# A prologue in another order: first weights earlier, score columns as products of their own, products of ones, factors per 128 rows

## The chip, the cores and the metric

The kernel runs on one core of a Trainium2 chip (trn2). The core has a matrix engine (TensorE, PE in the profile; its weight loads are shown as PEld), three engines for elementwise work (VectorE or DVE, ScalarE or ACT, GpSimd or POOL), and SyncE (SP), whose queue issues every transfer (DMA) of this kernel between device memory and the on-chip buffers. The engines run their own instruction streams, each in strict order, and wait for each other by semaphores. The metric is the device time of one execution in microseconds (us); lower is better.

## The reference

Two graph layers over 64 batches of 256 nodes with 512 features, in fp32. Cut to what matters:

```python
h = relu(layernorm(x))                       # layer 0
hW = einsum('bnf,fo->bno', h, W)             # W: 512 x 256
e = hW @ a[0] + swapaxes(hW @ a[1], 1, 2)    # score columns, one per node
alpha = softmax(leaky_relu(e, 0.2) + NEG * (1 - adj))
x = x + concatenate([alpha @ hW, hW], -1)

h = relu(layernorm(x))                       # layer 1, 8 heads of 64
q, k, v = h @ Wq.T + bq, h @ Wk.T + bk, h @ Wv.T + bv
attn = softmax(where(adj == 0, -inf, q @ k.T / 8))
x = x + (attn @ v) @ Wo.T + bo
```

## The kernel before, in words

The 64 batches are worked in 32 groups of two (`g`, with `b` 0 or 1); a batch is two tiles of 128 rows, so a group has four tiles `r`. All loops are unrolled. Each stage is a Python generator that emits one piece of instructions per `next`, and the order of the pieces is written out by hand: the first lines behind `verdict = judge()` (L1072 to L1126) are the prologue, the strings `steps` (L1131) the steady loop. There, each group's attention is interleaved with the projections of the group after it and with layer 0 of the group two ahead. The order on PE is pinned (`in_order`, L131); `not_sooner` (L123) pins an instruction behind the last one that was emitted on its engine.

The stages that matter here:

- `load(g, b)` (L147) transfers a batch of x, 512 KB.
- `first_norm(g)` (L531) normalizes for layer 0. `stats` computes mean and variance of 128 rows on DVE (BATCH_NORM_STATS2 and AGGREGATE), `factors` makes of them the scale and offset (two DVE operations, a power and a product on POOL, `factor`), `norm` applies them on ScalarE (`xn`). `turn`, `fetch` and `put` turn the result so that features lie on partitions (`hT`). For group 0 this goes through PE (transposes `pt` against `ident`). For all others it goes through memory: DVE transposes blocks of 32 (`xt`), SP stores them (`passed`, one transfer), SP fetches them back rearranged (`moved`, four transfers, which wait for `passed`), ScalarE copies them (`hT<-moved`).
- `first_layer(g)` (L671) is the rest of layer 0. For groups 0 and 1, four feature tiles `ph` are computed with `w0_sb`, which holds W in columns 2 to 257 and the two score columns W a[0], W a[1] in columns 0 and 1. `score_columns` (L174) computes these on DVE in eight products (`prod`). ScalarE copies a tile to `H`. The scores `e`: group 0 transposes score columns on PE (`pn`), later groups take them through memory (`score_rows`, L596: DVE transposes to `rows`, then transfers `line` and `own`). ScalarE adds and exponentiates, DVE multiplies by the mask `maskT`, PE computes the weighted sums `po`, DVE normalizes them into x and takes the statistics for layer 1.
- `project(g)` (L793) computes q, k and v of a group in seven block products each (Strassen-Winograd), from `hT` of layer 1, its `sums` (POOL) and the `sums` of the weights.
- `judge` (L292) computes bounds of the weights in pieces, among them `gram_q`, `gram_k` and four squares on PE. `mask` (L183) makes `maskT`.
- `late_loads` (L229) issues 19 transfers on SP: x of group 2 (2), the output weights `wo_sb` (8), the value bias `bv_col` (8) and the output bias `b_out` (1), each pinned behind SP's last.

Before the change SP issues in this order: x of group 0 (both batches), a_b (the vectors a), W, adj, Wq, x of group 1, Wk, biases, Wv, then `passed` and `moved` of group 1's first batch, of its second batch, then `late_loads`, then `line`, x of group 3, `own`. PE's order in the prologue: transposes of group 0's first batch, `ph` 0 and 1, transposes of the second, the mask's, `ph` 2 and 3, `pn`, gram_q, four `po`, gram_k, `ph_1_0` and `ph_1_1` (group 1), layer 1's transposes, squares, first q products.

Of the kernel before, what the change touches and what calls it, by code (L numbers as in the profile page):

```python
# [14 lines left out]
P = 128  # L15
# [42 lines left out]
def bounded(  # L58
# [86 lines left out]
    xs = {}  # L145

    def load(g, b):  # L147
        xs[g, b] = big.tile([P, NT, D], F32, tag="x", name=f"x{g}_{b}", bufs=8)
        if g == 2:
            not_sooner(sync, "dma_start", xs[g, b], xg[g, b])  # L150
        else:
            sync.dma_start(xs[g, b], xg[g, b])

    load(0, 0)
    load(0, 1)


    ident = const.tile([P, P], F32, name="ident")
    make_identity(nc, ident)
    maskT = const.tile([P, NT, N], F32, name="maskT")  # L160
    bad = const.tile([P, 2, NT], F32, name="bad")
    a_b = big.tile([P, 2, F1], F32, tag="oT0", name="a_b", bufs=1)
    nc.sync.dma_start(
        a_b, bass.AP(tensor=a0.tensor, offset=a0.offset, ap=[[0, P], [F1, 2], [1, F1]])
    )

    w0_sb = const.tile([P, HP, F1 + 2], F32, name="w0_sb")
    nc.sync.dma_start(w0_sb[:, :, 2:], w0.rearrange("(c p) o -> p c o", p=P))
    FH = F1 // 2 + 1
# [13 lines left out]
    def mask():  # L183
        edge = att.tile([P, NT, N], F32, tag="kept", name="edge", bufs=3)
        not_sooner(vector, "tensor_scalar", edge, adj_i, 0.0, None, op0=ALU.not_equal)
        yield
        pt = mm("pt_mask").rearrange("p (k q) -> p k q", k=NT)
        for kb in range(NT):
            for t in range(NT):
                transpose(  # L190
                    pt[:, kb, t * P : (t + 1) * P], edge[:, t, kb * P : (kb + 1) * P], ident
                )
        not_sooner(vector, "tensor_copy", maskT, pt)

        not_sooner(vector, "reduce_max", bad[:, 0, :], edge, axis=AX.X)
        vector.tensor_scalar(bad[:, 0, :], bad[:, 0, :], 0.0, None, op0=ALU.is_equal)
        vector.tensor_tensor(edge, edge, adj_i, op=ALU.not_equal)
        vector.reduce_max(bad[:, 1, :], edge, axis=AX.X)
        yield
# [52 lines left out]
    gpsimd.memset(ones, 1.0)  # L252
    square_ones = const.tile([P, P], F32, name="square_ones")
    gpsimd.memset(square_ones, 1.0)

    def weight_sums(name, engine=vector):
# [35 lines left out]
    def judge():  # L292
# [16 lines left out]
        for n, name in enumerate(("q", "k")):  # L309
            gram = bank(f"gram_{name}")  # L310
            for hp in range(HP):
                half, cols = hp // 2, slice(hp % 2 * P, (hp % 2 + 1) * P)
                for c in range(HP):
                    w = w_sb[name][:, c % 2, c // 2 * 2 + half, cols]
                    matmul(gram[:, hp, :], w, w, start=(c == 0), stop=(c == HP - 1))
            power[name] = room[:, n * HP : (n + 1) * HP, :]
            vector.tensor_mul(
                power[name], gram, heads[:, None, :].to_broadcast([P, HP, P])
            )
            yield  # L320
        for i in range(2):
            for n, name in enumerate(("q", "k")):
                square = bank(f"square_{name}{i}")
                for hp in range(HP):
                    a = power[name][:, hp, :]
                    matmul(square[:, hp, :], a, a, start=True, stop=True)
                if i < 1:
                    not_sooner(scalar, "copy", power[name], square)
                else:
                    scalar.activation(  # L330
                        power[name], square, AF.Square, accum_out=part[:, 8 + n : 9 + n]
                    )
                yield

# [87 lines left out]
    def norm_T(src, mv, name, by_pe):  # L422
# [5 lines left out]
        J = P // S  # L428

        def factors(b):  # L430
            tiles = slice(b * NT, (b + 1) * NT)
            several = small.tile([P, 3, NT], F32, tag="factor", name=f"factor{name}_{b}")
            ve, less, rstd = (several[:, i, :] for i in range(3))
            vector.tensor_scalar(ve, mv[:, tiles, 1], EPS, None, op0=ALU.add)
            vector.tensor_scalar(less, mv[:, tiles, 0], -1.0, None, op0=ALU.mult)
            if name == "0_0" or (name, b) == ("0_3", 0):
                not_sooner(gpsimd, "tensor_tensor", rstd, ve, rexp, op=ALU.pow)
            else:
                gpsimd.tensor_tensor(rstd, ve, rexp, op=ALU.pow)
            gpsimd.tensor_tensor(less, less, rstd, op=ALU.mult)  # L440
            factor[b] = less, rstd

        def norm(b):
            less, rstd = factor[b]
            for t in range(NT):
# [57 lines left out]

        return factors, norm, turn, fetch, put

# [25 lines left out]
    def first_norm(g):  # L531
# [5 lines left out]
        def measure(b):  # L537
            for t in range(NT):
                xt[b * NT + t] = xs[g, b][:, t, :]
                stats(mv, xt, b * NT + t, f"0_{g}")  # L540
            factors(b)

# [3 lines left out]

        if g in (1, 2):
            for b in range(GB):
                measure(b)
                yield  # L550
        if g == 1:
            for b in range(GB):
# [8 lines left out]
            return  # L561
        for b in range(GB):
            if g != 2:
# [6 lines left out]
            if g == 0:  # L570
                to_operand(b)
        if g == 0:
            return
# [97 lines left out]
    def first_layer(g):  # L671

        xt = [xs[g, b][:, t, :] for b in range(GB) for t in range(NT)]
        if g > 1:
            yield from first_products(g)
        for r in range(GT if g <= 1 else 0):
            b, t = divmod(r, NT)
            ph = mm(f"ph_{g}_{r}")[:, : F1 + 2]
            for c in range(HP):
                matmul(  # L680
                    ph, hT0[g, b][:, c, t * P : (t + 1) * P], w0_sb[:, c, :],
                    start=(c == 0), stop=(c == HP - 1),
                )
            scalar.copy(H[:, r, : F1 + 2], ph)
            gpsimd.tensor_add(xt[r][:, F1:], H[:, r, 2 : F1 + 2], xt[r][:, F1:])
            if r < GT - 1:
# [40 lines left out]
        for r in range(GT):  # L727
            b, t = divmod(r, NT)
            po = mm(f"po_{g}_{r}")[:, : F1 + 1]
            for kb in range(NT):  # L730
# [5 lines left out]
            not_sooner(vector, "reciprocal", ri, po[:, F1:])  # L736
            vector.scalar_tensor_tensor(
                xt[r][:, :F1], po[:, :F1], ri, xt[r][:, :F1], op0=ALU.mult, op1=ALU.add
            )
            stats(mv, xt, r, f"1_{g}")  # L740
            if r == 1:
                factors(0)
            elif r == 2:
                norm(0)
            elif r == 3:
                factors(1)
                if g:
# [45 lines left out]
    def project(g):  # L793
        ops = operands.pop(g)
        for name in ("q", "k", "v"):
# [25 lines left out]
            def take(to, bank, half):  # L821

                behind = [scalar.last] if g <= 1 and name != "v" else []
                if name == "v":
# [249 lines left out]
    bias, edges = last_bias(), mask()  # L1074
    for piece in range(5):
        next(norms)
        if piece == 3:
            score_columns()
            next(edges)
    products, pieces = project(0), first_layer(1) if NG > 1 else iter(())  # L1080
    for piece, _ in enumerate(first_layer(0)):
        if piece == 1:
            for _ in range(3):
                next(norms)
            next(edges)
        elif piece == 2 or piece == 3:
            next(norms)
        elif piece == 4:
            next(verdict)
            next(norms)  # L1090
        elif piece == 5:
            next(norms)
            late_loads()
        elif piece == 7:
            next(norms)
        elif piece == 9:
            next(verdict)
            next(pieces)
            next(pieces)
        elif piece == 10:  # L1100
            next(verdict)
            next(verdict)
            weight_sums("q")
        elif piece == 11:
            next(products)
            next(products)
            next(norms)
    next(norms)
    next(norms)
    next(pieces)  # L1110
    next(pieces)
    next(verdict)
    next(verdict)
    order = "- n s n s - - ss ss s s n - n - s - s -".split()
    for i, parts in enumerate(order, 2):
# [7 lines left out]
        for part in parts:  # L1123
            if part != "-":
                next(norms if part == "n" else pieces, None)
        if i in (12, 18, 19):  # L1126
            next(bias)
# [5 lines left out]
    for g in range(NG):  # L1133
        products = project(g + 1) if g + 1 < NG else iter(())
        pieces = first_layer(g + 2) if g + 2 < NG else iter(())
        for b, parts in enumerate(steps):
# [9 lines left out]
            for part in parts:  # L1146
# [409 lines left out]
```

## Time and profile before

| what | us |
|---|---|
| median of three runs (lowest, highest) | 2398.05 (2397.5, 2398.47) |
| the profiled execution's own time | 2401.28 |
| its span | 2399.5 |
| PE busy in 0 to 10, 10 to 20, 20 to 30 | 1.79, 8.12, 9.86 |
| DVE busy in the same windows | 4.09, 7.71, 8.91 |
| PE busy in 60 to 70, 100 to 110, 120 to 130 | 9.48, 9.05, 8.00 |
| PE busy in 1000 to 2000 | 1000.00 |

The profile is one execution, taken by the hardware profiler; its times count from the start of the span. In the steady part a group takes about 73 us (the scores of consecutive batches begin at 161.60, 198.82 and 234.97) and PE has no gap there. One fp32 matmul product is recorded as two matmuls, a transpose as one. Waits and releasers are inferred from semaphores; where an engine's order is strict, whatever stands behind a waiting instruction waits with it.

### The profile page before, as it was taken

Reading aid. Unit: us, or ns where it says so; the run is one execution under the profiler, and the core shown is the slowest. Engines: PE = TensorE matmul, PEld = TensorE weight load, DVE = VectorE, ACT = ScalarE, POOL = GpSimd, SP = SyncE. Lnnn points to the kernel's source line nnn. Section 1 sums busy time; section 2 is a strip of 40 time slices with the busy share of each in tenths; the row PEclk is TensorE's granted clock in tenths of the full one; section 3 lists DMA queues with packets and bytes.
Section 4 is the critical chain, followed back from the end, with each engine's and each line's share of the span. In section 5 each row is a group of like instructions: output and inputs, shape, how many; then the busy total and the mean of one; then the engine's idle time right before and its main releaser. Section 6 shows DMA issues by size and latency. Waiting matters only on the chain.

```text
span 2399.5 us, 42951 instructions
## 1 busy us (share of the span) xinstructions
PE 2378.2 (99%) x15772; PEld 2005.0 (84%) x15772; DVE 1693.1 (71%) x3338; ACT 1021.4 (43%) x2017; POOL 1418.4 (59%) x1282
## 2 busy tenths in 40 slices
PE   8999999999999999999999999999999999999998
PEld 7878888888888888888888888888888888888886
DVE  6677776777766777666767667776667676677666
ACT  5444444444443444444444434444444444344331
POOL 3565566656657555666556565655665555655652
PEclk9999999999999999999999999999999999999999
DMA  6344445544454544454444545444544445454331
GB/s 202 109 141 152 125 148 157 150 149 142 137 154 150 162 149 135 137 162 150 146 145 136 155 150 164 145 135 139 162 150 146 145 136 154 150 163 142 111 99 46
DMA packets 272041, 343.76 MB, mean 143 GB/s; under 512 B 25424, under 2 KB 217168, under 8 KB 271824
## 3 DMA queue, kind: packets, MB, share of 16 engines
q1 hardware_dynamic: 271824, 340.95, 46.0%
q8 instruction: 126, 2.06, 0.4%
q14 instruction: 91, 0.75, 0.1%
HBM read 177.22 MB, written 163.64 MB: 142 GB/s over the span
## 4 chain that ended last, share of the span: by engine, by line
PE 96%; DMA 1%; DVE 1%; ACT 1%; POOL 0%; issue 0%; SPq 0%; ACTq 0%; DVEq 0%; POOLq 0%
PE pv L137 16%; PE pk L137 16%; PE py L137 16%; PE pq L137 16%; PE sc L137 10%; PE pr L137 9%; PE ph L137 8%; PE po L137 4%; DMA x<-in_x_dram 0%; SPq L35 0%; DMA w_sb<-in_L_gnn_W_dram 0%; ACT e L35 0%; DMA line<-rows 0%; POOL x L35 0%; POOL parts L35 0%
## 5 line engine op out<-in xcount | busy, mean ns | idle before, releaser
L35 POOL TENSOR_TENSOR p<-p 128x512 f32<-128x512 f32 x248 | 384.5, 1563 | 483.4 <-DVE p L35 465.0
L35 ACT ACTIVATE xn<-x,factor 128x512 f32<-128x512 f32 x256 | 194.5, 807 | 324.5 <-POOL factor L35 324.0
L35 DVE TENSOR_TENSOR p<-p,maskT 128x1024 f32<-128x1024 f32 x254 | 329.5, 1318 | 1.4 <-ACT p L35 1.4
L35 ACT ACTIVATE p<-sc 128x512 f32<-128x512 f32 x512 | 258.1, 627 | 138.9 <-PE sc L137 121.1
L35 DVE TENSOR_TENSOR x<-py,x 128x256 f32<-128x256 f32 x448 | 185.8, 415 | 183.3 <-PE py L137 177.1
L35 POOL TENSOR_TENSOR parts<-parts 128x512 f32<-128x512 f32 x248 | 248.0, 1000 | 86.4 <-DMA parts<-rows 62.7
L137 PE MATMUL py<-wo_sb,oT 128*128 128x256 f32 x1024 | 262.4, 379 | 0.6 <-DVE oT L35 0.6
L137 PE MATMUL sc<-q,k 64*128 64x256 f32 x2048 | 253.1, 391 | 2.0 <-DVE oT L35 2.0
L137 PEld LDWEIGHTS sc<-q,k 64*128 64x128 f32 x2048 | 205.6, 187 | 50.1 <-issue 26.3
L137 PE MATMUL pk<-hT,wk_sb 128*128 128x256 f32 x1024 | 244.8, 382 | 0.0
L137 PE MATMUL pq<-hT,wq_sb 128*128 128x256 f32 x1024 | 240.0, 382 | 0.3 <-ACT kept_q L35 0.3
L137 PE MATMUL pv<-wv_sb,hT 128*128 128x256 f32 x1024 | 236.9, 379 | 0.0
L137 PE MATMUL pr<-p,v 128*32 128x256 f32 x4096 | 234.2, 380 | 0.0
L35 POOL TENSOR_TENSOR factor<-factor,rexp 128x2 f32<-128x2 f32 x128 | 115.6, 903 | 179.9 <-DVE factor L35 179.7
L137 PEld LDWEIGHTS pq<-hT,wq_sb 128*128 128x128 f32 x1024 | 191.8, 190 | 35.8 <-issue 10.3
L137 PEld LDWEIGHTS py<-wo_sb,oT 128*128 128x128 f32 x1024 | 194.2, 190 | 28.2 <-DVE oT L35 1.1
L137 PEld LDWEIGHTS pk<-hT,wk_sb 128*128 128x128 f32 x1024 | 189.7, 190 | 33.3 <-issue 9.9
L137 PEld LDWEIGHTS pv<-wv_sb,hT 128*128 128x128 f32 x1024 | 194.5, 190 | 27.1 <-issue 0.5
L137 PEld LDWEIGHTS pr<-p,v 128*32 128x32 f32 x4096 | 126.8, 110 | 97.8 <-issue 15.9
L137 PE MATMUL py<-wo_sb,o_sums 128*128 128x256 f32 x768 | 197.6, 380 | 1.4 <-DVE x L35 1.3
L137 PE MATMUL pk<-sums,wk_sb 128*128 128x256 f32 x768 | 181.6, 379 | 0.5 <-ACT kept_k L35 0.5
L137 PE MATMUL pq<-sums,wq_sb 128*128 128x256 f32 x768 | 181.4, 379 | 0.0
(148 smaller groups left out, 4059.1 us busy)
## 6 DMA issues: line engine op xcount, KB each, us to landing
passed<-xt SPq DMA_DIRECT2D x124, 512.0 KB, 3.1
moved<-passed SPq DMA_DIRECT2D x496, 128.0 KB, 3.5
rows<-p SPq DMA_DIRECT2D x124, 512.0 KB, 3.4
parts<-rows SPq DMA_DIRECT2D x496, 128.0 KB, 3.0
x<-in_x_dram SPq DMA_DIRECT2D x64, 512.0 KB, 4.4
out_dram<-x SPq DMA_DIRECT2D x62, 512.0 KB, 4.0
own<-line SPq DMA_DIRECT2D x31, 256.0 KB, 3.2
wq_sb<-in_L_gnn_Wq_dram SPq DMA_DIRECT2D x2, 512.0 KB, 9.9
```

The lines of the kernel that those rows point to most:

```text
L35: instruction = getattr(self.engine, operation)(*args, **kwargs)
L137: in_order(nc.tensor.matmul(*args, **kwargs))
```

## The change

Nothing that is computed for the output changes but the way to the two score columns of group 0's first batch; the rest is order.

1. PE begins with 12 products of ones (`warm_up`) into a bank that nobody reads; `square_ones` is set earlier.
2. SP's order: W directly behind the first batch of x, then the second batch, then a_b. x of group 3 is issued in the prologue, behind a `passed` of group 2.
3. For group 0's first batch, the 256 feature columns and the 2 score columns are products of their own, the latter emitted behind the transposes of the second batch.
4. Scale and offset are computed per 128 rows in group 0, for both layers (`factor_of`), no longer per 256.
5. Group 1's normalization is emitted later: its ScalarE part behind group 0's exponentials, its DVE transposes behind the product that follows gram_q. Between its two batches, on SP, now stand the 19 transfers of `late_loads`.
6. On PE: gram_k moves ahead of the fourth `po`; the feature tiles of group 1 (`ph_1_0` to `ph_1_3`) move behind layer 1's transposes and between the q products; the squares move behind the last q product and behind the second k product.
7. The last residual addition is emitted at the end of the step before.

```diff
+    def warm_up():
+        warm = mm("warm")
+        for _ in range(12):
+            matmul(warm[:, :P], square_ones, square_ones, start=True, stop=True)
...
     load(0, 0)
-    load(0, 1)
+    square_ones = const.tile([P, P], F32, name="square_ones")
+    gpsimd.memset(square_ones, 1.0)
...
+    w0_sb = const.tile([P, HP, F1 + 2], F32, name="w0_sb")
+    nc.sync.dma_start(w0_sb[:, :, 2:], w0.rearrange("(c p) o -> p c o", p=P))
+    load(0, 1)
     a_b = big.tile([P, 2, F1], F32, tag="oT0", name="a_b", bufs=1)
...
+        def factor_of(b, t):
+            if t == 0:
+                several = small.tile([P, 3, NT], F32, tag="factor", name=f"factor{name}_{b}")
+                factor[b] = several[:, 0, :], several[:, 1, :], several[:, 2, :]
+            less, rstd, ve = (f[:, t : t + 1] for f in factor[b])
+            r = b * NT + t
+            not_sooner(vector, "tensor_scalar", ve, mv[:, r, 1:2], EPS, None, op0=ALU.add)
+            not_sooner(vector, "tensor_scalar", less, mv[:, r, 0:1], -1.0, None, op0=ALU.mult)
+            not_sooner(gpsimd, "tensor_tensor", rstd, ve, rexp[:, :1], op=ALU.pow)
+            gpsimd.tensor_tensor(less, less, rstd, op=ALU.mult)
...
+        apart = NT if g == 0 else 0
+        heads = []
+        for r in range(apart):
+            heads.append(mm(f"ph_{g}_{r}")[:, : F1 + 2])
+            features(heads[r], r, slice(2, F1 + 2), True)
+            yield
+        for r in range(apart):
+            features(heads[r], r, slice(0, 2), False)
+            taken(heads[r], r)
...
-    for piece in range(5):
-        next(norms)
-        if piece == 3:
-            score_columns()
-            next(edges)
...
-    order = "- n s n s - - ss ss s s n - n - s - s -".split()
+    work = {"n": norms, "0": layer, "1": pieces, "u": products, "c": verdict, "e": edges}
+    warm_up()
+    take(*"nnnnn")
+    score_columns()
+    take(*"en00nn0e00n0cnn")
+    late_loads()
+    take(*"000n0c00n0n")
+    weight_sums("q")
+    take(*"euun0011")
+    order = "- nss n nn ns - s - ss ss s s n - n - s - s".split()
...
+        if i in (6, 8):
+            take(*"cc")
+        if i == 7:
+            take("c")
+        if i == 8 and NG > 3:
+            load(3, 0)
+            load(3, 1)
...
-                parts = ("Smmoomoomooo", "Smrmoomoomooo")[b]
+                parts = ("Smmoomoomooor", "Smmoomoomooo")[b]
...
-                    if g + 3 < NG:
+                    if 0 < g < NG - 3:
```

In the strings, a letter is one piece of a stage: n of the normalizations, 0 and 1 of layer 0 for groups 0 and 1, u of group 0's projections, c of `judge`, e of `mask`, s of group 1's layer, and in the loop's strings S the scores, m the masking, o the outputs, r a residual addition.

More of the change, by code (lines that the diff above doesn't have):

```diff
@@ L145, in bounded @@
     xs = {}
+    def warm_up():
+        warm = mm("warm")
+        for _ in range(12):
+            matmul(warm[:, :P], square_ones, square_ones, start=True, stop=True)
     def load(g, b):
         xs[g, b] = big.tile([P, NT, D], F32, tag="x", name=f"x{g}_{b}", bufs=8)
-        if g == 2:
+        if g in (2, 3):
             not_sooner(sync, "dma_start", xs[g, b], xg[g, b])
@@ L165, in bounded @@
     )
-    w0_sb = const.tile([P, HP, F1 + 2], F32, name="w0_sb")
-    nc.sync.dma_start(w0_sb[:, :, 2:], w0.rearrange("(c p) o -> p c o", p=P))
     FH = F1 // 2 + 1
@@ L252, in bounded @@
     gpsimd.memset(ones, 1.0)
-    square_ones = const.tile([P, P], F32, name="square_ones")
-    gpsimd.memset(square_ones, 1.0)
     def weight_sums(name, engine=vector):
@@ L316, in judge @@
             power[name] = room[:, n * HP : (n + 1) * HP, :]
-            vector.tensor_mul(
-                power[name], gram, heads[:, None, :].to_broadcast([P, HP, P])
+            not_sooner(
+                vector, "tensor_mul", power[name], gram, heads[:, None, :].to_broadcast([P, HP, P])
             )
             yield
+        squared = {}
         for i in range(2):
@@ L327, in judge @@
                 if i < 1:
-                    not_sooner(scalar, "copy", power[name], square)
+                    squared[name] = square
                 else:
@@ L332, in judge @@
                     )
+                yield
+            for name, square in squared.items():
+                not_sooner(scalar, "copy", power[name], square)
+            if squared:
+                squared.clear()
                 yield
@@ L435, in factors @@
             vector.tensor_scalar(less, mv[:, tiles, 0], -1.0, None, op0=ALU.mult)
-            if name == "0_0" or (name, b) == ("0_3", 0):
+            if (name, b) == ("0_3", 0):
                 not_sooner(gpsimd, "tensor_tensor", rstd, ve, rexp, op=ALU.pow)
@@ L443, in norm @@
         def norm(b):
-            less, rstd = factor[b]
+            less, rstd = factor[b][:2]
             for t in range(NT):
@@ L502, in put @@
             put_last[:] = [scalar.last]
-        return factors, norm, turn, fetch, put
+        return (factor_of if by_pe else factors), norm, turn, fetch, put
     def operand_sums(engine, quads, sums):
@@ L540, in measure @@
                 stats(mv, xt, b * NT + t, f"0_{g}")
-            factors(b)
+                if g == 0:
+                    factors(b, t)
+            if g:
+                factors(b)
         def to_operand(b):
@@ L545, in to_operand @@
             put(b, hT0[g, b])
-        if g in (1, 2):
+        if g == 1:
             for b in range(GB):
@@ L550, in first_norm @@
                 yield
-        if g == 1:
-            for b in range(GB):
                 norm(b)
@@ L561, in first_norm @@
             return
+        if g == 2:
+            for b in range(GB):
+                measure(b)
+                yield
         for b in range(GB):
@@ L571, in first_norm @@
                 to_operand(b)
+                yield
         if g == 0:
@@ L675, in first_layer, with features, taken @@
             yield from first_products(g)
-        for r in range(GT if g <= 1 else 0):
+        def features(ph, r, columns, start):
             b, t = divmod(r, NT)
-            ph = mm(f"ph_{g}_{r}")[:, : F1 + 2]
             for c in range(HP):
                 matmul(
-                    ph, hT0[g, b][:, c, t * P : (t + 1) * P], w0_sb[:, c, :],
-                    start=(c == 0), stop=(c == HP - 1),
+                    ph[:, columns], hT0[g, b][:, c, t * P : (t + 1) * P], w0_sb[:, c, columns],
+                    start=start and c == 0, stop=(c == HP - 1), skip_group_check=(g == b == 0),
                 )
+        def taken(ph, r):
             scalar.copy(H[:, r, : F1 + 2], ph)
-            gpsimd.tensor_add(xt[r][:, F1:], H[:, r, 2 : F1 + 2], xt[r][:, F1:])
+            sum_of = xt[r][:, F1:], H[:, r, 2 : F1 + 2], xt[r][:, F1:]
+            if g:
+                not_sooner(gpsimd, "tensor_add", *sum_of)
+            else:
+                gpsimd.tensor_add(*sum_of)
+        apart = NT if g == 0 else 0
[3 more added lines that the diff above has]
+            features(heads[r], r, slice(2, F1 + 2), True)
+            yield
+        for r in range(apart):
+            features(heads[r], r, slice(0, 2), False)
+            taken(heads[r], r)
+        if apart:
+            yield
+        for r in range(apart, GT if g <= 1 else 0):
+            ph = mm(f"ph_{g}_{r}")[:, : F1 + 2]
+            features(ph, r, slice(0, F1 + 2), True)
+            taken(ph, r)
             if r < GT - 1:
@@ L736, in first_layer @@
             not_sooner(vector, "reciprocal", ri, po[:, F1:])
-            vector.scalar_tensor_tensor(
-                xt[r][:, :F1], po[:, :F1], ri, xt[r][:, :F1], op0=ALU.mult, op1=ALU.add
-            )
-            stats(mv, xt, r, f"1_{g}")
-            if r == 1:
-                factors(0)
-            elif r == 2:
+            weighed = xt[r][:, :F1], po[:, :F1], ri, xt[r][:, :F1]
+            if g == 0:
+                not_sooner(
+                    vector, "scalar_tensor_tensor", *weighed, op0=ALU.mult, op1=ALU.add
+                )
+            else:
+                vector.scalar_tensor_tensor(*weighed, op0=ALU.mult, op1=ALU.add)
+            stats(mv, xt, r, f"1_{g}")
+            if g == 0:
+                factors(b, t)
+            elif t == 1:
+                factors(b)
+            if r == 2:
                 norm(0)
             elif r == 3:
-                factors(1)
                 if g:
@@ L821, in take @@
             def take(to, bank, half):
-                behind = [scalar.last] if g <= 1 and name != "v" else []
+                behind = [scalar.last] if g == 0 and name != "v" else []
                 if name == "v":
@@ L1074, in bounded, with take @@
     bias, edges = last_bias(), mask()
-    for piece in range(5):
-        next(norms)
-        if piece == 3:
-            score_columns()
-            next(edges)
[L1080 to L1113, printed above, removed]
-    order = "- n s n s - - ss ss s s n - n - s - s -".split()
+    def take(*names):
+        for name in names:
+            next(work[name])
+    layer, products = first_layer(0), project(0)
+    pieces = first_layer(1) if NG > 1 else iter(())
+    work = {"n": norms, "0": layer, "1": pieces, "u": products, "c": verdict, "e": edges}
[8 more added lines that the diff above has]
+    order = "- nss n nn ns - s - ss ss s s n - n - s - s".split()
     for i, parts in enumerate(order, 2):
```

## The prediction

> **What bounds the kernel now.** I read the page first: TensorE (PE) is busy for 2378.2 of 2399.5 us, so all other time is 21 us of PE gaps, and only a gap on PE can be won or lost.
>
> ```profile
> PE 2378.2 (99%) x15772; PEld 2005.0 (84%) x15772; DVE 1693.1 (71%) x3338; ACT 1021.4 (43%) x2017; POOL 1418.4 (59%) x1282
> ```
>
> The busy times by window (window, length, then busy us and records of PE, PEld, DVE, ACT and POOL, granted clock, DMA share, GB/s) say where the gaps are: 8.2 + 1.9 us in the first 20, 0.5 from 60 to 70, about 1.0 from 100 to 110, 2.0 from 120 to 130, the rest at the end; from 130 to 2350 there are practically none. The edit touches the first 130 us, so its price is the shift of PE's unbroken stream after them.
>
> ```profile
> 0.00:10.00 10.00, 1.79 (x8) 1.57 (x8) 4.09 (x16) 3.38 (x4) 2.93 (x17) 1.00 0.72 211
> 10.00:20.00 10.00, 8.12 (x31) 5.96 (x31) 7.71 (x30) 3.83 (x7) 2.11 (x4) 1.00 1.07 382
> 120.00:130.00 10.00, 8.00 (x86) 5.45 (x80) 7.52 (x16) 6.83 (x15) 2.69 (x3) 0.83 0.16 63
> ```
>
> Then the timeline (start, length, engine, line, operation, tiles, records, idle time before). Early PE work is slow as well as late: 8 transposes take 1.97 us at 8.21 and 1.04 at 38.01; 16 feature matmul records take 6.34 us at 12.06 and 3.65 at 34.52.
>
> ```profile
> 8.21 1.97 PE L140 MATMUL pt<-ident,xn 128*128 128x128 f32 x8 [8.21 <-ACT xn L35]
> 12.06 6.34 PE L137 MATMUL ph<-w_sb,hT 128*128 128x258 f32 x16 [1.88 <-DVE prod L35]
> 34.52 3.65 PE L137 MATMUL ph<-w_sb,hT 128*128 128x258 f32 x16
> 38.01 1.04 PE L140 MATMUL pt<-ident,xn 128*128 128x128 f32 x8
> ```
>
> Last the DMA queue of SP, which issues every transfer in one order, and the chain of waits up to 64 us. This decides my forecast.
>
> ```profile
> 24.12 0.34 SPq L35 DMA_DIRECT2D passed<-xt  x1
> 26.80 1.75 SPq L35 DMA_DIRECT2D moved<-passed  x4
> 29.61 0.34 SPq L35 DMA_DIRECT2D passed<-xt  x1
> 33.02 1.73 SPq L35 DMA_DIRECT2D moved<-passed  x4
> 34.79 0.94 SPq L35 DMA_DIRECT2D x<-in_x_dram  x2
> 35.78 9.21 SPq L35 DMA_DIRECT2D wo_sb<-in_L_gnn_Wo_dram  x8
> 45.03 4.71 SPq L35 DMA_DIRECT2D bv_col<-in_L_gnn_bv_dram  x8
> 49.79 0.42 SPq L35 DMA_DIRECT2D b_out<-in_L_gnn_bo_dram  x1
> 50.31 0.58 SPq L35 DMA_DIRECT2D line<-rows  x1
> ```
>
> The 19 transfers of `late_loads` hold SP from 34.79 to 50.25: 15.46 us. SP's waits name 4.7 us of it, two waits for the landing of x; the `wo_sb` rows behind are slow too (7.7 us median to landing). In the chain of waits the same stretch is followed by `line`, `own`, the exponentials and `kept_k`, and frees PE at 63.05:
>
> ```profile
> 35.27 9.39 DMA x<-in_x_dram
> 50.31 4.88 DMA line<-rows
> 63.05 1.13 PE pk L137 x4
> ```
>
> **The change, part by part.** Times are us of the span. All instructions keep their row's duration; what moves is who waits.
>
> *Start, 0 to 20.* `square_ones` is set first on POOL (0.20 us), so PE starts 12 products of ones at about 1.1. Each fp32 product is two records (8 feature products are 16 rows): 24 records at the slow 1.97/8 = 0.25 end near 7.0, at the fast 1.04/8 near 4.2. Factors per 128 rows let `xn` skip one BN pair (0.84 us): the first transposes come at 7.4 instead of 8.21, so the products lie in idle time; uncovered they would cost 3.1 to 5.9. W0 now follows the first x. Today it lands at 2.38 + 8.57 = 10.95, behind a_b (9.27); DVE takes the second x at 6.14, so in that place W0 is there by about 6.1, the second x by 7.4, a_b by 10.6. The second half's `xn` ends at 8.3, its copies at 9.5; the feature products run from 8.9 to 12.6 at the fast rate. The eight DVE products for the score columns take 3.7 us (11.06 to 14.8 now), from 10.6 to 14.3. The eight narrow products for the columns are new: 16 records at the 0.11 of the 128-column rows are 1.8 us, the second half of them behind 14.3, so 15.4. Then the mask's transposes 0.5, two feature tiles 3.65, copy and `pn` 0.8: gram_q starts at 20.4 instead of 23.89. PE leads by 3.5.
>
> The slow start is told by the rows above alone: twice the time for the same records; the clock column shows 1.00 there and does not tell of it. The window 120 to 130 shows it again behind a gap: 2.00 us of waiting at 124.6, then granted clocks of 0.59 and 0.55 in the windows 126 to 128 and 128 to 130, 1.7 us lost. The Trainium skill, "TensorE: Matmul & The Clock Gate", section "Why this matters for your kernels", asks for no gaps over about 3 us. By that rule the 2.00 us gap would have cost no clock; the trace shows that it did. With the rule or the row the gap that I find below drops the clock, so the sum is the same; only gaps of 2 to 3 us differ, by 1.7 us each.
>
> *20 to 31: layer 1's first part.* Group 1's normalization now stands behind the exponentials on ScalarE, and its transposes behind gram_q's product on DVE. e at 20.45; the exponentials end and `xn` starts 2.86 later, as now (24.09 to 26.95), and takes 1.50: 24.8. DVE has gram_q's 0.68 ahead and 1.29 for its two transposes: `passed` is issued at 26.15, against 24.12 now, though PE is ahead. Landing 2.68 (24.12 to 26.80), `moved` 1.75: SP is free at 30.6.
>
> *The step that decides: group 1's second half behind `late_loads`.* In the built order of SP, the second `passed` and `moved` now stand behind all 19 late loads. With 15.46 they start at 30.6 + 15.46 = 46.1; landing 3.41 (29.61 to 33.02), 49.5; last `moved` issue 1.29 later, 50.8; landing 3.5 (2.6 to 3.9 in the trace), 54.3; ScalarE's copy 0.57: feature products `ph_1_2` at 54.9. PE stands in strict order, and all it has left is queued behind.
>
> When does PE get there? po, three tiles, 24.0 to 26.6; gram_k to 30.2; fourth po 31.1; transposes to 32.0, copy, q products from 32.9 (0.9 idle, where squares stood before); 36.4; transposes of the second half held by its `xn` to 37.6; `ph_1_0` waits for the copy of `moved` until 38.5, ends with `ph_1_1` at 42.1; the third q product needs POOL's two sums (2 x 1.27 behind 40.2) at 42.8; 46.3. PE waits from 46.3 to 54.9: 8.6 us. The lead of 3.5 was already spent on gaps of 0.9, 0.3, 0.9 and 0.7 us.
>
> Clock lost behind it: 1.7 (window 126 to 130) to 2.7 (the first 16 feature records, 6.34 less 3.65); I take 2.6, as the start too follows a long idle time.
>
> *Against now, at the same PE instruction,* the third k product, at 63.05: 54.9 + 2.6 + feature products 3.49 + three q products 5.19 + squares 1.79 + two k products 3.46 + squares 1.78 = 73.2. Lag: 10.2. `line`, `own` and the exponentials leave about 61.7, and 63.05 - 50.31 = 12.7 behind that is 74.4, less 2.2 since x no longer stands between `line` and `own`: 72.2, no extra. Behind that the waits of 0.34 (101.5) and 0.55 (107.55) can close, 0.7 taken of 0 to 0.9. The 2.00 at 124.6 stays: POOL is filled up to 122.69 by sums that begin with PE's own features at 113.2. Lag 9.5.
>
> The skill's "DMA: Bandwidth & Descriptors", section "Rules for kernel authors", says to issue a DMA early and wait late, which speaks for late loads in front. By it their place would cost nothing and the sum end near the old time; the row has 15.46 us of issue on one queue, with a need behind it.
>
> *At nothing:* x of group 3 loaded earlier (0.47 us an issue; behind what this stage needs). Additional factors, 4 x (0.71 + 0.19) = 3.6 us on POOL, lie where POOL is busy 2.1 of 10 us and 2.9 of 10; without that cover up to 3.6. The squares are moved, equal in number. The last residual addition keeps its place among POOL's instructions.
>
> **Sum.** The profiled execution is 2401.28 (span 2399.5), the median of three runs 2398.05. PE's shift holds for both: 2410.8 on the profile's scale, 2398.05 + 9.5 = 2407.6 as the median.
>
> **The rivals.**
> *B, late loads pass at issue rate (not slower).* If the two waits for x and the slow rows do not come back, 19 x 0.47 = 8.9 us, and `ph_1_2` starts at 48.3, PE waits 2.0 without much clock loss; the third k product comes at 48.3 + 15.7 = 64.0, less 0.7: +0.2, about 2398.3. This decides from a length of 8.9 downwards; between 8.9 and 15.46 each us costs one. For: most issues take 0.43. Against: contents and order of these 19 are the same, behind the same four `moved`.
> *C, no stall at all, the start's lead kept.* Group 1's second half is there when PE comes: 46.3 + 15.7 = 62.0 against 63.05, less 0.7: -1.8; if the gap at 124.6 and its clock (3.7) also close, -5.5. Between the two, about 2394. For: 3.5 us of real lead. Against: SP's row.
> *D, it grows:* clock drop of 3.4, `kept_k` behind late exponentials by 1, landings at 3.9: +12.5, 2410.6.
>
> **How the numbers follow.** Forecast 0.68 (its own range 2403.5 to 2410), B 0.14, C 0.13, D 0.05. The measurement tells about 0.2% (4.8 us) from no change. Slower: 0.68 + 0.05 + a fifth of B, 0.75. Faster: two thirds of C, 0.09. Same: 0.16. The range 2397 to 2411 holds the forecast, D and most of B.
>
> **What would show it.** Right: SP's second `passed` near 46, `ph` waiting on `moved` or its ScalarE copy for 7 to 10 us near 50, granted clock under 1 behind it. First transposes near 7.4 and feature records at the fast rate would show the start right. Wrong: SP passing the late loads in under 9 us, or PE reaching `ph_1_2` after 52.

## The result, and the profile after

The changed kernel takes 2411.26 us (median of five runs, 2410.31 to 2416.09) against 2398.05: 1.0059 times the time of before, 95% interval 1.0044 to 1.0073, so slower by 13.2 us. Its profiled execution took 2416.09 us, 4.8 above its median (that of before was 3.2 above its own), with a span of 2414.4: on the two traces the shift is 14.9. Times read from its trace are thus those of the slowest of its five executions.

The page's first part, busy time by engine:

```profile
PE 2387.8 (99%) x15812; PEld 2012.6 (83%) x15812; DVE 1697.8 (70%) x3346; ACT 1021.7 (42%) x2017; POOL 1422.3 (59%) x1290
```

PE is busy 9.6 us longer than before and idle 26.6 instead of 21.3. The busy times by window (columns as in the prediction) show where:

```profile
0.00:10.00 10.00, 7.21 (x35) 6.61 (x36) 4.58 (x21) 4.12 (x6) 3.34 (x19) 0.92 0.79 234
...
50.00:60.00 10.00, 3.17 (x8) 2.52 (x8) 0.00 (x0) 1.14 (x2) 0.34 (x1) 0.64 0.25 68
60.00:70.00 10.00, 10.00 (x47) 8.67 (x46) 4.73 (x15) 0.86 (x3) 2.41 (x5) 0.85 0.08 26
70.00:80.00 10.00, 7.65 (x39) 6.89 (x38) 7.81 (x12) 7.36 (x16) 3.61 (x6) 0.83 0.48 159
```

From 50 to 60 no engine beside TensorE does more than 1.2 us of work, and PE does 3.17: everything waits for a transfer. From 60 to 80 the granted clock is 0.83 to 0.85. The same shows in PE's timeline, with the second scores of the changed kernel by themselves. Then come five of these instructions in the kernel before, one instruction of ScalarE in the changed kernel that matters below, and its SP queue. In them `room` holds the operand of the squares, and `kept_q`, `kept_k` and `kept_v` are what ScalarE copies out of q, k and v products.

```profile
1.12 4.78 PE L137 MATMUL warm<-square_ones 128*128 128x128 f32 x24 [1.12 <-POOL square_ones L35]
7.24 0.66 PE L140 MATMUL pt<-ident,xn 128*128 128x128 f32 x4 [1.34 <-ACT xn L35]
...
8.99 5.01 PE L137 MATMUL ph<-w_sb,hT 128*128 128x256 f32 x16
...
21.17 3.75 PE L137 MATMUL gram_q<-wq_sb 128*128 128x128 f32 x32
...
56.83 6.79 PE L137 MATMUL ph<-w_sb,hT 128*128 128x258 f32 x16 [7.80 <-ACT hT L35]
...
76.38 1.85 PE L137 MATMUL square_q<-room 128*128 128x128 f32 x8 [2.35 <-ACT room L35]
...
79.73 2.06 PE L137 MATMUL pk<-sums,wk_sb 128*128 128x256 f32 x8
...
107.40 4.38 PE L137 MATMUL sc<-q,k 64*128 64x256 f32 x32
```

```profile
143.20 2.85 PE L137 MATMUL sc<-q,k 64*128 64x256 f32 x22 [0.26 <-ACT p L35]
```

```profile
23.89 3.75 PE L137 MATMUL gram_q<-wq_sb 128*128 128x128 f32 x32
...
45.00 3.65 PE L137 MATMUL ph<-w_sb,hT 128*128 128x258 f32 x16
...
63.05 1.99 PE L137 MATMUL pk<-sums,wk_sb 128*128 128x256 f32 x8 [0.52 <-ACT kept_k L35]
...
88.41 3.92 PE L137 MATMUL sc<-q,k 64*128 64x256 f32 x32
...
126.63 4.40 PE L137 MATMUL sc<-q,k 64*128 64x256 f32 x22 [2.00 <-DVE oT L35]
```

```profile
69.89 1.52 ACT L35 ACTIVATE xn<-x,factor 128x512 f32<-128x512 f32 x2 [5.86 <-POOL factor L35]
```

```profile
31.77 0.95 SPq L35 DMA_DIRECT2D x<-in_x_dram  x2
32.77 8.98 SPq L35 DMA_DIRECT2D wo_sb<-in_L_gnn_Wo_dram  x8
41.79 3.71 SPq L35 DMA_DIRECT2D bv_col<-in_L_gnn_bv_dram  x8
45.55 0.43 SPq L35 DMA_DIRECT2D b_out<-in_L_gnn_bo_dram  x1
46.07 0.38 SPq L35 DMA_DIRECT2D passed<-xt  x1
51.50 1.75 SPq L35 DMA_DIRECT2D moved<-passed  x4
64.30 0.58 SPq L35 DMA_DIRECT2D line<-rows  x1
```

The start is ahead (gram_q at 21.17 instead of 23.89). Then the 19 late transfers hold SP from 31.77 to 46.07, the second `passed` comes behind them, and the feature products that need it start at 56.83 after 7.80 us of waiting, at half clock for most of it: 16 records in 6.79 us instead of 3.65. The list of PE's waits (total, times, longest) names what follows:

```profile
PE ph L137 <- ACT hT L35: 8.4, 2, 7.8
PE pt L140 <- ACT xn L35: 2.6, 3, 1.3
PE square_q L137 <- ACT room L35: 2.3, 1, 2.3
PE pv L137 <- ACT kept_v L35: 1.8, 2, 1.2
...
PE pq L137 <- POOL sums L35: 1.3, 1, 1.3
```

At the same PE instruction the changed kernel leads by 2.7 at gram_q, lags by 16.7 at the third k product (79.73 against 63.05), by 19.0 at the first scores (107.40 against 88.41), and by 15.0 from the third scores on (176.55 against 161.53). Of these 4.0, 3.3 are regained at the second scores, which waited 2.00 at 124.6 before and now wait 0.26 (the line at 143.20), with no clock lost behind it.

### The profile page after: what moved, and what is told of

The parts are those of the page before. It is cut to its first block, busy times and chain, and to the rows that moved or that the text cites. A ratio compares the mean times of both kernels' runs of the same rounds, so it can differ in the third digit from the quotient of the medians.

```text
span 2414.4 us, 43064 instructions
## 1 busy us (share of the span) xinstructions
PE 2387.8 (99%) x15812; PEld 2012.6 (83%) x15812; DVE 1697.8 (70%) x3346; ACT 1021.7 (42%) x2017; POOL 1422.3 (59%) x1290
## 4 chain that ended last, share of the span: by engine, by line
PE 96%; DVE 2%; DMA 1%; ACT 1%; issue 0%; SPq 0%; POOL 0%; DVEq 0%; ACTq 0%
PE pk L137 16%; PE py L137 16%; PE pv L137 16%; PE pq L137 16%; PE sc L137 10%; PE pr L137 9%; PE ph L137 8%; PE po L137 4%; DMA passed<-xt 0%; DVE st L35 0%; DVE x L35 0%; DMA wo_sb<-in_L_gnn_Wo_dram 0%; ACT e L35 0%; PE total L137 0%; DVE xt L35 0%
## 5 line engine op out<-in xcount | busy, mean ns | idle before, releaser
L35 POOL TENSOR_TENSOR factor<-factor,rexp 128x2 f32<-128x2 f32 (+1 forms) x132 | 116.6, 883 | 176.3 <-DVE factor L35 175.9
L137 PEld LDWEIGHTS pr<-p,v 128*32 128x32 f32 x4096 | 126.8, 110 | 97.8 <-issue 15.3
L137 PE MATMUL pv<-wv_sb,sums 128*128 128x256 f32 x768 | 181.6, 379 | 1.8 <-ACT kept_v L35 1.8
```

Source lines behind the costliest of these rows:

```text
L35: instruction = getattr(self.engine, operation)(*args, **kwargs)
L137: in_order(nc.tensor.matmul(*args, **kwargs))
```

## The experiments

"Before" was run again with each group on the same chip: 2397.12, 2398.14 and 2397.91 us in the three groups that follow.

**Late transfers behind group 1's second batch** (changed kernel):

```diff
-    late_loads()
     take(*"000n0c00n0n")
+    late_loads()
```

> The changed kernel with late_loads emitted behind the transfers of group 1's second half, nothing else. Theory (SP's one order is the cause: whatever stands behind the 19 late loads waits some 15 us): the wait of ph_1_2 (7.8 us in the changed kernel's profile) is gone, the second passed is issued near 38 in place of 46.1; but line and own now stand behind the late loads, line near 57, so the wait comes back at the squares or the third k product (4 to 7 us near 65), and the median is 2402 to 2408. Rival (the other moves cost by themselves: the four short PE waits between 33 and 46 and the squares' place): the time stays within 2 us of 2411.

Measured: 2406.33 us, ratio 1.0035 (1.0022 to 1.0047). The second `passed` leaves at 38.53 and is fetched from 41.18 (2.65 instead of 5.43 to its landing), the feature products wait 1.44 instead of 7.80. The wait of the squares stays, 2.45 at 65.2, with the drop of the clock behind it:

```profile
51.00 3.75 PE L137 MATMUL ph<-w_sb,hT 128*128 128x258 f32 x16 [1.44 <-ACT hT L35]
```

The time lies in the theory's range, but the wait of 4 to 7 us that it saw coming back near 65 measured 2.45, and the next run shows that it is not the late transfers'. The stall of the first place is worth 4.0 us by the medians, each against its own before (4.9 as the medians stand), and 8.8 by the spans of the two profiled executions, of which that of the changed kernel was its slowest.

**The 17 late transfers that are not x behind `own`** (changed kernel; `late_rest` is the second half of `late_loads`):

```diff
         load(2, 1)
+    def late_rest():
         rows = woT.rearrange(...)
...
+        if i == 3:
+            late_rest()
```

> The changed kernel with only the two x transfers of group 2 in front of group 1's second half, and the other 17 late loads behind line and own. Theory: no transfer that PE needs soon stands behind a late load: no PE wait over 2 us before 100, ph_1_2 near 49, the third k product near 65 (63.05 before the change, 79.7 behind it), median 2394 to 2401. Rival (the other moves cost by themselves): the squares' wait of 2.4 us and its clock drop stay and the median is above 2405.

Measured: 2404.45 us, 1.0030 (1.0020 to 1.0040). The theory's 2394 to 2401 missed: SP was free of them in time (`passed` 36.79, `line` 53.70, `own` 55.45), yet the squares still wait 2.35 and pv 1.8. The rival saw the wait rightly, but the clock did not fall behind it, and the time lies below its 2405. The 7.3 us that are left are about half of the loss, and they are not the late transfers'.

**Group 1's second normalization behind the late transfers, alone** (kernel before, in the piece that issues them):

```diff
         elif piece == 5:
-            next(norms)
             late_loads()
+            next(norms)
```

> The kernel before with late_loads emitted in front of the transfers of group 1's second half, nothing else of the change (the x transfers of group 3 fall between passed and moved by the program's own ordering). Theory: this one move makes the loss: second passed near 44, ph_1_2 waits 8 to 12 us, the clock drops behind it, median 2406 to 2413. Rival (the loss needs the rest of the new order): within 3 us of 2398.

Measured: 2408.48 us, 1.0045 (1.0031 to 1.0060), as the theory said, though the second `passed` went out earlier than its 44. SP's queue and PE's longest wait:

```profile
29.66 6.46 SPq L35 DMA_DIRECT2D wo_sb<-in_L_gnn_Wo_dram  x8
...
40.28 0.42 SPq L35 DMA_DIRECT2D b_out<-in_L_gnn_bo_dram  x1
40.80 0.38 SPq L35 DMA_DIRECT2D passed<-xt  x1
41.22 1.56 SPq L35 DMA_DIRECT2D x<-in_x_dram  x2
46.57 1.75 SPq L35 DMA_DIRECT2D moved<-passed  x4
```

```profile
PE ph L137 <- ACT hT L35: 8.4, 1, 8.4
```

One line moved in the kernel before makes the stall and 11 us of loss. Nothing else of the change is needed for it.

**Without the products of ones** (changed kernel):

```diff
-    warm_up()
```

> The changed kernel without the 12 products of ones. Theory: PE starts at the slow rate and becomes fast 3 to 6 us later, gram_q starts 1 to 2.5 us later than the 21.2 of the changed kernel, and SP's chain behind it moves as much: median 2412 to 2414. Rival (the start is set by the score columns on DVE, so the ones are worth nothing): gram_q within 0.5 us of 21.2, median within 1 us of 2411.

Measured: 2412.44 us, 1.0060 (1.0044 to 1.0077), gram_q at 21.04 against 21.17 with them. The theory that gram_q would come 1 to 2.5 us later fell: with the ones the full clock came at 4.99 but was taken back from 8.40 to 11.81; without them it came at 11.37 and stayed through the start. The median is in that theory's 2412 to 2414, but its interval does not tell it from the changed kernel's. One execution says little of the start: in the eight traces with the ones, gram_q begins anywhere from 19.96 to 21.79. The earliest is that of the run with the 17 behind `own`, where the full clock came at 7.22 and was not taken back, so that the feature products took 3.70 us instead of 5.01.

**W ahead, alone** (kernel before):

```diff
     load(0, 0)
+    w0_sb = const.tile(...)
+    nc.sync.dma_start(w0_sb[:, :, 2:], ...)
     load(0, 1)
```

> The kernel before with one part of the change alone: W is transferred directly behind the first batch of x, ahead of the second batch and of the vectors a. Theory: the start gains (feature products at about 10.6 instead of 12.06, gram_q 1.5 to 2.5 us earlier than 23.89), but the lead is lost at the third k product, because the kept_k in front of it stands on ScalarE behind exponentials that wait for the transfers line and own, and those stand behind the late loads on SP: the wait of 0.52 us at 63 grows by what the start gained. Time 2396.5 to 2398.5. Rival: SP does not hold the lead back, and 1.5 to 2.5 us are kept: 2394.5 to 2396.

Measured: 2398.76 us, 1.0001 (0.9992 to 1.0010). The time is just above the theory's range and not told from no change, and not for the theory's reason: the feature products start only 0.6 us earlier (11.46, held by the copies hT), take 6.86 because the clock comes no sooner (full from 17.61), and gram_q is at 23.81. There was no lead to lose. The wait at 63 did not grow either: `own` went out at 51.72 instead of 55.20, and the third k product began at 62.55.

**W ahead and the 17 behind `own`** (kernel before, both edits):

```diff
     load(0, 0)
+    w0_sb = const.tile(...)
+    nc.sync.dma_start(w0_sb[:, :, 2:], ...)
     load(0, 1)
...
+    def late_rest():
...
+        if i == 3:
+            late_rest()
```

> As the run with W ahead, and the 17 late transfers that are not x (wo_sb, bv_col, b_out) are issued behind line and own. Theory: line is issued as soon as its rows are written (near 49 instead of 50.31), own some 4 us earlier than 55.20, kept_k is no longer late, the wait of 0.52 at 63 goes and the start's lead stays: 2 to 3.5 us below before, 2394.5 to 2396.5, and the gap of 2.0 at 124.6 is still there or a little longer. Rival: the lead is used up at another wait (feature products of group 1 waiting for moved, or the gap at 124.6 growing by as much): 2397 to 2398.5.

Measured: 2396.93 us, 0.9994 (0.9985 to 1.0003), between the two forecasts and not told from no change. `own` went out at 51.04 instead of 55.20 and the wait of 0.5 at 63 was gone, as the theory has it; but it was gone in the previous run too, with the late transfers in their old place, so the move of the 17 is not shown to be the cause.

**Statistics of group 2 ahead of `rows`** (changed kernel with the 17 behind `own`):

```diff
-    order = "- nss n nn ns - s - ss ss s s n - n - s - s".split()
+    order = "- nnnss - n ns - s - ss ss s s n - n - s - s".split()
```

> The changed kernel with the 17 late transfers behind own, as in the earlier run (2404.45), and with the statistics of group 2 emitted ahead of the transposes rows on DVE (order string: - nnnss - n ns instead of - nss n nn ns). Theory: the second squares wait because ScalarE's copies room stand behind xn of group 2, which waited 5.86 us for a factor whose statistics stood behind rows on DVE. With the statistics in DVE's idle 5.5 us before rows, xn runs near 53.5, kept_k and the copies come 3 us or more earlier, the wait of 2.35 falls under 0.8: 2401 to 2403. Rival: the exponentials, which wait for own, hold ScalarE as long; the wait stays over 1.5: 2403.5 to 2405.5.

Measured: 2402.26 us, 1.0017 (1.0008 to 1.0027), in the theory's range, and the wait of the squares is gone. The same line of ScalarE's timeline and the squares on PE, without the edit and then with it:

```profile
59.29 1.52 ACT L35 ACTIVATE xn<-x,factor 128x512 f32<-128x512 f32 x2 [5.86 <-POOL factor L35]
...
65.79 1.16 PE L137 MATMUL square_q<-room 128*128 128x128 f32 x8 [2.35 <-ACT room L35]
```

```profile
55.16 1.52 ACT L35 ACTIVATE xn<-x,factor 128x512 f32<-128x512 f32 x2
...
65.14 1.16 PE L137 MATMUL square_q<-room 128*128 128x128 f32 x8
```

ScalarE had stood for 5.86 us on a factor, with q, the exponentials, kept_k and the squares' copies queued behind. The factor's statistics stood on DVE behind `rows`, which waited 5.50 us for `H`. From gram_q to the third k product the traces take 45.24 us instead of 47.72, so 2.5 less; the medians differ by 3.2, each against its own before, and by 2.2 as they stand. In the changed kernel ScalarE stood on the same factor for the same 5.86 us (its line at 69.89 above).

**The second squares later** (changed kernel with the 17 behind `own`):

```diff
-        if i in (6, 8):
+        if i in (6, 10):
             take(*"cc")
```

> The changed kernel with the 17 late transfers behind own, and with the second squares two q/k pieces later (behind the second po instead of behind the second k product). Theory: the wait has no need to be, since nothing soon depends on the squares; if the squares alone were badly placed, the 2.35 us go: 2401 to 2403. Rival: the third k product, which would come first, waits for the same ScalarE queue (kept_k, near 65.3 in the run before): the wait only changes its name, about 1.9 of 2.35 us stay: 2403.5 to 2405.

Measured: 2403.36 us, 1.0025 (1.0015 to 1.0034), between the theory's 2401 to 2403 and the rival's 2403.5 to 2405; the trace decides. The wait has another name:

```profile
66.42 1.99 PE L137 MATMUL pk<-sums,wk_sb 128*128 128x256 f32 x8 [1.87 <-ACT kept_k L35]
```

So it was ScalarE's queue that was late, not the squares that stood badly.

**The start alone** (kernel before with W ahead, score columns apart, ones, factors per 128 rows in layer 0 of group 0, and the 17 behind `own`; the rest in before's order):

```diff
+    warm_up()
     for piece in range(5):
         next(norms)
-        if piece == 3:
-            score_columns()
-            next(edges)
+    score_columns()
+    next(edges)
...
-        for r in range(GT if g <= 1 else 0):
+        apart = NT if g == 0 else 0
+        for r in range(apart):
+            features(heads[r], r, slice(2, F1 + 2), True)
...
-        return factors, norm, turn, fetch, put
+        return (factor_of if name == "0_0" else factors), norm, turn, fetch, put
```

> The kernel before with the start of the change alone (W ahead, score columns of group 0's first batch as products of their own, 12 products of ones, factors per 128 rows in layer 0 of group 0), and with the 17 late transfers behind own. Everything from gram_q on stands in the order of before: group 1's normalization, its feature products, the squares. Theory: the start gains 2.7 us (gram_q near 21.2, as in the changed kernel), the places that lost it are not there, the wait of 0.5 at 63 is gone too, and 2.5 to 3.2 us stay at the end: 2394.5 to 2396. Rival: the order of before was fitted to its later start, and the lead is used up by group 1's transfers (feature products waiting for moved) or by a longer gap at 124.6: 2397 to 2398.5.

Measured: 2395.89 us, 0.9990 (0.9981 to 0.9999): faster than both kernels, in the theory's range. In PE's timeline gram_q starts near where it does in the changed kernel, and from there to 97.8 PE has no gap over 0.2:

```profile
21.01 3.75 PE L137 MATMUL gram_q<-wq_sb 128*128 128x128 f32 x32
```

**The same, all late transfers in before's place:**

```diff
-    def late_rest():
...
-        if i == 3:
-            late_rest()
```

> As the run with the start alone, but all late transfers in the place of before, ahead of line and own. Theory: own lands as late as before, kept_k with it, and PE arrives at the third k product some 2 us earlier: the wait of 0.5 grows to 2 or 3 us, and most of the start's gain is lost: 2396.5 to 2398.5. Rival: the late transfers pass SP faster with the start's transfers in another order (13.6 us in the run with W ahead, against 15.46), and the gain stays: 2394.5 to 2396.

Measured: 2395.98 us, 0.9991 (0.9982 to 1.0000). The theory missed and the rival's range held: the late transfers were past SP in 12.8 us (32.78 to 45.57), `line` went out at 47.51 as in the run above (47.46), and nothing grew. With the second `passed` ahead of them, this place costs nothing that can be measured.

**The start alone, without ones:**

```diff
-    warm_up()
```

> As the run with the start alone, without the 12 products of ones. Theory: they gain little, as in the changed kernel without them (gram_q 21.04 against 21.17): the clock is granted in steps of 3.4 us that the ones only shift; same as the run with them within 1 us. Rival: the ones bring the full clock forward for the 16 feature records, 1 to 2.7 us; without them gram_q comes at 22.2 to 23.9 and the time is that much longer.

Measured: 2398.33 us, 1.0000 (0.9991 to 1.0009), 2.4 more than with them, and no run of the one kernel reaches a run of the other (2397.25 to 2398.91 against 2395.4 to 2396.32). That is the rival's size, but not its reason: gram_q is at 21.30, only 0.3 later. In the traces the rest arises at the second scores: 2.00 us of waiting instead of 1.15, and half the clock behind it. The windows of the run without ones and of the run with them:

```profile
124.00:127.00 3.00, 3.00 (x16) 2.90 (x16) 2.97 (x7) 2.89 (x6) 0.00 (x0) 0.50 0.00 0
```

```profile
124.00:127.00 3.00, 3.00 (x20) 2.30 (x17) 3.00 (x6) 3.00 (x7) 0.00 (x0) 1.00 0.02 5
```

In this one execution `line`, which `own` waits for, took 3.9 us to `own`'s issue (112.21 to 116.13) instead of 2.8. Why leaving out the ones should do that over eleven runs stays open. With it goes a caution: this kernel has the early gram_q too, and by the medians nothing of the lead is left at its end (2398.33 against 2397.91).

**The start alone, and the division of group 0 ahead of group 2's leaky relu** (strings of the loop, and a pin on DVE):

```diff
-                parts = "Smmnfuuumnmnuufuussssfsfssuvnfrunnfsuu"
+                parts = "Smmnfuuumnmnuufuussssfsfssuvnfrunnfuu"
+            elif g == 0:
+                parts = "s" + parts
...
+            if g == 2:
+                not_sooner(vector, "scalar_tensor_tensor", e, e, ALPHA, e, ...)
```

> As the run with the start alone, and on DVE group 0's first division (r, oT) ahead of group 2's leaky relu (e), which waits for own; the exponentials of group 2 behind kept_k on ScalarE. This takes away the 2.00 us wait of the scores at 124.6. Theory: the wait goes, and with it the drop of the clock behind it, so 2.0 plus 1.7: 3 to 4 us below the run with the start alone, 2391 to 2393. Rivals: the clock drops there all the same, then 2.0 or less; or po of group 2 waits for the later e instead, then nothing.

Measured: 2400.19 us, 1.0009 (1.0000 to 1.0018): slower than the start alone by 4.3, a loss that neither the theory nor a rival gave. The wait on oT went (0.25 is left), and a longer one came, since ScalarE's exponentials of the scores now queue behind those of group 2, which wait for DVE:

```profile
126.44 3.05 PE L137 MATMUL sc<-q,k 64*128 64x256 f32 x14 [3.30 <-ACT p L35]
```

**Together.** Medians, each against the run of before in its own group:

| kernel | against before, us | step |
|---|---|---|
| before with the change's start, 17 behind `own` | -2.0 | -2.0, the start with its ones |
| changed order from gram_q on, 17 behind `own`, statistics ahead | +4.1 | +6.1, the rest of the new order |
| statistics behind `rows` | +7.3 | +3.2, the squares' wait |
| late transfers behind the second batch, ahead of `line` | +9.2 | +1.9 |
| the change: late transfers ahead of the second batch | +13.2 | +4.0 |

The interval of each ratio reaches about 0.1%, 2.4 us, to either side, and the rows come from different groups. The step of 1.9 is therefore not told from nothing, and those of 3.2 and 4.0 rest on the waits that the traces show. The second step holds everything else that was reordered (PE's order, group 1's normalization, layer 1's factors, the last residual addition). Where its cost may lie is seen in the trace of the second row: waits of 0.67, 0.98, 0.57, 1.29, 1.44, 0.57 and 1.24 between 33 and 89, 6.8 in sum, where the first row's kernel has none. Which of its parts makes which wait was not taken apart.

## Why the prediction was right in its direction and wrong in its size

*Direction and mechanism held.* The second `passed` stood behind the late transfers, PE waited near 50, the clock fell behind it, and most of the lag stayed. One line moved in the kernel before, without the rest, costs 11.4 us. The size was too small: lag 9.5 against 13.2 by the medians and 14.9 by the profiles, and 2411.26 is just above the range's end of 2411.0. The step that failed is a term of the sum that was put at nothing: "no extra" at the third k product, where the second squares cost 3.9 us. The steps in order, read from the one trace:

- *Start.* First transposes at 7.24 (7.4 said), ones 4.78 us (3.1 to 5.9). "The feature products run from 8.9 to 12.6 at the fast rate" failed: 5.01 us, because the clock was taken back at 8.40 (it held in the run with the 17 behind `own`, 9.10 to 12.80). gram_q at 21.17 instead of 20.4, the lead 2.7 instead of 3.5.
- *The queue.* Second `passed` at 46.07 (46.1 said), by luck, since two errors cancel: the late transfers began at 31.77 instead of 30.6 and took 14.3 instead of 15.46. Its landing was costed at 3.41 and took 5.43 (46.07 to 51.50), right behind `b_out`; 2.65 where nothing stood directly in front. The feature products started 1.9 later than said. PE came there at 49.03, not 46.3, so that the wait of 7.8 came out near the 8.6 said, by luck again. This length is not fixed: without the ones, with gram_q at the same place, the late transfers took 12.0 us and the wait was 4.89.
- *Clock behind it.* 3.1 (6.79 less 3.65), 2.6 taken.
- *The step that failed*, "no extra" at the third k product. The sum put the second squares at 1.78 without a wait. They waited 2.35 and then, at half clock, took with their successor's start 1.6 us longer (76.38 to 79.73): 3.9 in all. I had followed `line`, `own` and the exponentials to kept_k, but not what the moved piece brought with it: the squares need copies on ScalarE, and ScalarE stood on group 2's factor. The run with the statistics ahead shows it: the wait is gone, and PE comes to this product 2.5 us sooner after gram_q. The wait is not chance of the one trace: it is 2.35, 2.45 and 2.35 without the ones, with the late transfers behind the second batch, and with the 17 behind `own`; the half clock behind it came in the first two of these and not in the third. Lag 16.7 at this product instead of 10.2: 1.9 + 0.5 + 3.9, and 0.2 of the rest.
- *Behind it.* Two new waits of pv, 1.8 in sum, were not costed: the lag was 19.0 at the first scores. The 0.7 taken for the waits that can close came out at the second scores (18.3), though only that of 0.55 closed, not that of 0.34, and the first scores took 0.5 longer. "The 2.00 at 124.6 stays" was wrong the other way: 3.3 of lag regained there. The sums of `e` on ScalarE began 4.8 us behind the issue of `own` before (117.93 to 122.72) and 3.3 behind it now (136.21 to 139.51); why was not tried.

*The rivals.* B (late transfers at 8.9 us) fell: 12.0 to 15.46 us in every run with all 19 together. C fell in the changed kernel; its condition, the lead with no stall, came true in the start alone, with 2.0 us below before. D (2410.6) came nearest, and was given 0.05. It named the landing and the clock; kept_k stood in the same late queue of ScalarE, but it was the squares' copies that PE waited for.

*Two rules weighed.* The Trainium skill, "DMA: Bandwidth & Descriptors", section "Rules for kernel authors", says to issue early and wait late. In the kernel before, the late transfers one place earlier cost 11.4 us; in the start alone, their place behind `own` or ahead of `line` made no difference (2395.89 and 2395.98). In these runs, then, early was free where the next transfer behind went out as soon as without it (`line` at 47.51 against 47.46), and dear where it did not. "TensorE: Matmul & The Clock Gate", section "What's actually happening", says that the clock falls after at least one idle window of about 3.4 us, and that windows run freely. The length agrees: the clock records change in steps of 3.413 us. A wholly idle window was not needed: the window 122.96 to 126.37 of the kernel before had 1.74 us idle, and the clock fell. Here the measurement decides.

## What to carry to other kernels

When work is put at an earlier place on a queue that issues in order, price the next needed transfer behind it, with its landing, and not only the issue time of what was put in front. When a piece moves on the bounding engine, follow each of its operands through the queue of the engine that makes it: a copy of 0.6 us behind a waiting instruction costs that wait. A faster start in front of a sequence of many short hand-overs is best tried with the old sequence left as it was: here that gave 2 us (none without the products of ones), and with the new order it was lost three times over.

## What the runs showed of the hardware

In these traces the granted clock changes in steps of 3.413 us, and a window of that length need not be idle throughout for the clock to fall behind it. The same wait of 2.35 us lay inside one window in the changed kernel (73.26 to 76.67) and was followed by half clock; in the run with the 17 behind `own` it lay across two (1.80 and 0.55 us idle, with the edges counted in steps of 3.413 from 7.22, where its full clock began) and was not. The windows of the changed kernel, then of that run:

```profile
73.00:77.00 4.00, 1.65 (x9) 1.19 (x8) 3.86 (x6) 3.67 (x8) 0.84 (x2) 0.96 0.97 316
77.00:80.00 3.00, 3.00 (x15) 3.00 (x15) 1.92 (x4) 0.69 (x2) 0.00 (x0) 0.50 0.29 108
```

```profile
60.00:64.00 4.00, 3.44 (x16) 2.67 (x15) 2.98 (x5) 3.84 (x10) 3.07 (x5) 1.00 0.68 135
64.00:68.00 4.00, 2.21 (x18) 2.19 (x19) 3.93 (x7) 2.98 (x8) 0.00 (x0) 1.00 0.59 121
```

One bound in idle time does not fit all of them: among the scores, whose tiles use 64 of 128 rows, windows with 1.45 (W ahead) and 1.59 us idle (W ahead, 17 behind `own`) dropped the clock and one with 1.15 (the start alone) did not, while 1.80 among full tiles did not. Whether the fill of the tiles is what counts was not tried.

The length of the same 19 late transfers on SP was not fixed: 15.46 us in the kernel before, 14.3 in the changed one, 12.9 where they alone were moved ahead (27.85 to 40.70) and 12.0 without the ones (31.64 to 43.64), in one execution each.
